# Four stacked graph layers on one core: the running maxima five pairs ahead, three blocks' softmax terms spread by TensorE, two PSUM banks for turned adjacency, and layer 1's buffers in other pools

## The chip, the cores and the metric

The kernel runs on one core of one Trainium2 chip. The metric is the device time of one execution in microseconds. Engine names are those of the profile: PE is TensorE's matmul and PEld its weight load, DVE is VectorE, ACT is ScalarE, POOL is GpSimd, SP is SyncE, which here only issues DMAs. A line number such as L326 is a line of the kernel before; the changed kernel's lines lie a few further down.

## The reference

Four residual graph layers over x (4096 x 256, float32) with one adjacency matrix adj (4096 x 4096, int32, about 0.8% ones). Each takes `h = relu(layernorm(x))`, computes a layer of h and adj, and adds it to x.

```python
# layer 0
Wh = h @ W
e = leaky(Wh @ a_src + (Wh @ a_dst).T, 0.2)
attn = softmax(where(adj > 0, e, -9e15), axis=1)
h_attn = attn @ Wh
# ... then a dense part: B, C, dt = split(Wh @ W_bcdt + b); gated MLPs of
# width 512 (fe1, fe2, W_hz, out_w, g1, g2), layer norms with gains and shifts
# layer 1
a = (adj == 1);  x += (a @ h / deg) @ W.T + b
# layer 2
h2 = h @ W
e = leaky(h2 @ a[:D] + (h2 @ a[D:]).T, 0.01)
x += elu(softmax(where(adj > 0, e, -1e12)) @ h2)
# layer 3
x += softmax(Q @ K.T + mask(adj + eye)) @ V
```

Layers 0 and 2 are additive attention: the logit of a row and a column is a leaky ReLU of one number per row plus one per column, masked by adj.

## The kernel before, in words

Rows and columns are cut into 32 tiles of 128. x stays in SBUF as `xs`. The code is written against a tile framework: buffers come from pools with a fixed count, an instruction waits by semaphore for the buffer and the data that it needs, and a scheduler orders each engine's instructions from the program order and the pools. An engine executes its instructions in its own fixed order, so a waiting instruction holds all that are behind it.

**Turned adjacency (layer 0).** A unit is a piece of 128 rows by 1024 columns of adj. `load` fetches it by POOL as bf16 (L479; 512 KB are read as int32, 256 KB written); `fresh` turns it with eight TensorE transposes into a PSUM bank (`cT`, L488), and ACT maps it with an exponential to a code in SBUF (`turned`, L493). There are 128 units. The codes also go to DRAM (`codesT`, L513), from where layers 1 to 3 read them back. `FRESH = 8` says how many pairs ahead of the running pair units are turned.

**Additive attention (class `Attention`, layers 0 and 2).** Rows are processed in blocks: layer 0 in two blocks of two row tiles and then seven of four, layer 2 in eight of four. Columns go in pairs of two tiles, 16 pairs a block (`PPB`). Three things happen for every pair, in one loop (`run`):

- `reach(n + PPB + LEAD)` takes, for the *next* block, the running minimum of code minus column term over two column tiles (L273, L275 on DVE). It gives each row's largest logit. After the block's last pair `top` turns it on TensorE (L289), computes two numbers a and b per row (L292 to L297 on DVE), turns those (`abT`, L299), and spreads them over all partitions: by a write to DRAM and a read back as a broadcast on SP's queue (L313, L314), or, for block 0 of layer 0 alone, by small matmuls against `picks` (L307) and two copies.
- `logits` makes the pair's logits y: two DVE operations with a and b (L326; ACT copied b to PSUM at the block's start, L324), then POOL subtracts the code (L330).
- Three pairs later (`lag`), ACT applies exp (L357) and PE accumulates: y as weights against `v`, which holds a column of ones, Wh and the column terms (L368). A 4-row pair is eight products. At a block's end DVE takes reciprocals of the row sums (L376), and ACT and DVE write the quotient (layer 0: `finish0`, L441 and L443; layer 2: `finish2`, L913 to L924).

`LEAD = 3` is the number of pairs by which the reaches run ahead: a block's last reach is done that many pairs before its first logits.

**Preparation of layer 0.** x arrives in eight loads of four tiles, alternating between SP and ACT (L605). `weights` loads W and the vectors a by ACT's queue and computes the columns W·a on DVE (L236). `block0` then centers x (L620, L624), takes statistics, turns x on TensorE (L145), multiplies by W (L154), and does the first reaches; beside it, adjacency units are loaded and turned.

**Dense part.** Eight blocks of 512 rows. Its late weights are loaded by `keep` in the last attention block into slots of the pool `l0_kept`, in the groups and at the pairs listed in `LATE`. Its intermediates lie in the pool `l0_d`. The last steps of a block are layer norm, POOL's multiply by ln_g (L861) and addition (L862).

**Layer 1.** `gather(t)` reads codes (L988), DVE turns them to 0/1 masks `eq` (L995) and PE multiplies (L1006). ACT counts degrees from adjacency loads (L173, L180). `reach2` prepares layer 2: `weights2` loads layer 2's weights by POOL, and its columns are again computed at L236. Pools that are opened here are laid over those that the dense part has closed.

**Layer 2** runs the same class over codes read from DRAM (`stored`, L901) into seven buffers, with two buffers for the tiles of its finish. **Layer 3** (from about 2021 us on) is ordinary attention.

Of the kernel before, what the change touches and what calls it, by code (L numbers as in the profile page):

```python
# [11 lines left out]
F32 = mybir.dt.float32  # L12
BF16 = mybir.dt.bfloat16
# [5 lines left out]
PSUM = bass.MemoryType.PSUM  # L19
DRAM = bass.MemoryType.DRAM  # L20

P = 128
# [19 lines left out]
def kernel(ctx: ExitStack, tc: tile.TileContext, w: dict, out: bass.AP):  # L42
    nc = tc.nc
    x, adj = w["x"], w["adj"]
    N, D = x.shape
# [146 lines left out]
    class Attention:  # L192
        def __init__(self, es, tag, slope, lag, n_y, blocks, turned, finish):
            self.tag, self.slope, self.lag, self.n_y = tag, slope, lag, n_y
            self.turned, self.finish = turned, finish
            self.blocks = [{"at": at, "n": n} for at, n in blocks]
            vp = es.enter_context(tc.tile_pool(name=f"{tag}_sd", bufs=1))
            self.sdst = vp.tile([P, NT], F32, name="sdst")
            self.cdst = vp.tile([P, NT], F32, name="cdst")
            self.own_dst, self.held = None, False  # L200
            self.ab_d = [
                dram.tile([2, n, P], F32, name=f"{tag}_ab_d{k}") for k, (_, n) in enumerate(blocks)
            ]
            self.picks = None
            self.small = es.enter_context(tc.tile_pool(name=f"{tag}_small", bufs=4))
            self.row_p = es.enter_context(tc.tile_pool(name=f"{tag}_rows", bufs=2))
            self.ps_run = es.enter_context(tc.tile_pool(name=f"{tag}_run", bufs=1, space=PSUM))
            self.ps_top = es.enter_context(tc.tile_pool(name=f"{tag}_top", bufs=1, space=PSUM))
# [9 lines left out]
        def weights(self, wp, work, wm, a_srcs, eng):  # L218
# [5 lines left out]
            a2 = wp.tile([P, 2 * D], F32, name="a2")  # L224
            at = 0
            for a in a_srcs:
                n = a.shape[0]
                eng.dma_start(
                    out=a2[:, at : at + n],
                    in_=a.rearrange("s o -> (s o)").partition_broadcast(P),  # L230
                )
                at += n
            for k in range(KD):
                for v in range(2):
                    junk = work.tile([P, D], F32, tag="junk", name="junk")
                    nc.vector.tensor_tensor_reduce(  # L236
                        junk, w2[:, k, 0:D], a2[:, ts(v, D)], 1.0, 0.0, ALU.mult, ALU.add,
                        w2[:, k, D + v : D + v + 1],
                    )
            self.w2 = w2  # L240
# [40 lines left out]
        def top(self, b):  # L281
# [139 lines left out]
    LEAD = 3  # L421
    FIRST = 8
    FRESH = 8
    with ExitStack() as l0:
# [10 lines left out]
        with ExitStack() as es:  # L435
# [13 lines left out]
            def turned_of(k, q):  # L449
# [4 lines left out]
            att = Attention(es, "l0", 0.2, 3, 8, cuts, turned_of, finish0)  # L454
# [4 lines left out]
            att.picks = picks.tile([4, 4, P], F32, name="picks")  # L459
            nc.vector.tensor_copy(  # L460
                att.picks,
                ident[0:4, 0:4].rearrange("k (v o) -> k v o", o=1).broadcast_to([4, 4, P]),
# [3 lines left out]
            ps_c = es.enter_context(tc.tile_pool(name="ps_c", bufs=1, space=PSUM))  # L466
# [41 lines left out]
            def ahead(n):  # L508
# [84 lines left out]
            with ExitStack() as ps_:  # L593
# [6 lines left out]
                load(4)  # L600
                att.weights(
                    wp, work, w["L0_gnn_W"], (w["L0_gnn_a_src"], w["L0_gnn_a_dst"]), nc.scalar
                )
                for b in range(NB):
                    (nc.scalar if b % 2 else nc.sync).dma_start(  # L605
# [4 lines left out]
                def block0(b):  # L610
# [16 lines left out]
                    rs = rstd_of(small, mv, BT, "pl")  # L627
                    load(2 * b + 6)
# [19 lines left out]
        with ExitStack() as es:  # L648
            d = es.enter_context(tc.tile_pool(name="l0_d", bufs=1))
# [54 lines left out]
            def hidden(z, g, b):  # L704

                zT = d.tile([P, KI, BW], F32, tag="zT", name="zT", bufs=2)
# [13 lines left out]
            def dense(b):  # L720
# [45 lines left out]
                t1 = d.tile([P, BT, DI], F32, tag="t", name="t", bufs=2)  # L766
# [20 lines left out]
                sz = d.tile([P, KI, BW], F32, tag="sz", name="sz")  # L787
# [20 lines left out]
                henh = d.tile([P, BT, D], F32, tag="henh", name="henh")  # L808
# [16 lines left out]
                comb = d.tile([P, 2 * KD, BW], F32, tag="comb", name="comb")  # L825
# [10 lines left out]
                t2 = d.tile([P, BT, DI], F32, tag="t", name="t", bufs=2)  # L836
# [110 lines left out]
    with ExitStack() as es:  # L947
# [104 lines left out]
        def weights2():  # L1052
            att2.weights(one2, two2, w["L2_gnn_W"], (w["L2_gnn_a"],), nc.gpsimd)
# [287 lines left out]
```

## Time and profile before

| what | value |
|---|---|
| median of three runs | 2996.88 us (2996.64 to 3000.27) |
| profiled execution, its own time | 2998.89 us |
| its span, first to last instruction | 2997.0 us |
| busy PE / PEld | 2864.1 us (96%) / 2334.0 us |
| busy DVE / ACT / POOL | 1878.5 / 1282.4 / 954.4 us |
| mean granted TensorE clock | 0.989 |
| moved by DMA | 239.41 MB, 80 GB/s |

The stages in the span: preparation of layer 0 until 68 us, its two small blocks until 170, its seven large blocks until 624, the dense part until 1228, layer 1 until about 1530, layer 2's attention from 1538 to 2018, layer 3 to the end.

Busy time says which engine limits a stretch, a wait says which work an engine stood for; idle time of an engine that limits nothing costs nothing. Waits are listed with the waiting instruction, what released it, the sum in us, how often, and the longest. In the timeline a row is a run of like instructions: start, length, engine, line, operation, tiles, count, and in brackets the idle time before it and its releaser.

### The profile page before, as it was taken

The numbers are of one execution on the slowest core, as the hardware profiler recorded it, in microseconds if no ns is written. First come the engines' busy times: TensorE is split into PE (matmuls) and PEld (weight loads), VectorE is DVE, ScalarE is ACT, GpSimd is POOL, SyncE is SP. The second block draws the span as 40 slices with busy tenths as digits, with TensorE's granted clock in tenths as the row PEclk, the third lists the DMA queues.
The fourth block names the chain that finished last, engine by engine and source line by source line (L and its number), as shares of the span: only waits on it lengthen the run. The fifth ranks groups of instructions, "written<-read, shape, count | busy, mean of one in ns | idle before, by whom it ended". The sixth has DMA issues, their size and how long they took to land.

```text
span 2997.0 us, 35132 instructions
## 1 busy us (share of the span) xinstructions
PE 2864.1 (96%) x13357; PEld 2334.0 (78%) x13357; DVE 1878.5 (63%) x3456; ACT 1282.4 (43%) x1961; POOL 954.4 (32%) x718
## 2 busy tenths in 40 slices
PE   6989999999999999899999999999999999999999
PEld 5778888866555666687877788888888888888888
DVE  5877666425555554477688788646766566566653
ACT  5765656459997223793163444333212112111211
POOL 4666665534554333220044655550000000000000
PEclk9999999999999999999999999999999999999999
DMA  6966665245553000496332222101111111111100
GB/s 145 213 147 128 132 133 136 67 64 77 78 78 53 8 8 8 122 241 174 123 148 85 78 78 78 43 12 61 64 44 54 38 34 62 39 34 62 34 8 8
DMA packets 109473, 239.41 MB, mean 80 GB/s; under 512 B 10780, under 2 KB 31256, under 8 KB 100600
## 3 DMA queue, kind: packets, MB, share of 16 engines
q1 hardware_dynamic: 68936, 165.44, 15.9%
q0 software_dynamic: 37696, 69.11, 15.4%
q10 hardware_dynamic: 2672, 2.62, 0.3%
q8 instruction: 105, 1.72, 0.2%
q14 instruction: 64, 0.52, 0.1%
HBM read 266.42 MB, written 37.81 MB: 102 GB/s over the span
## 4 chain that ended last, share of the span: by engine, by line
PE 63%; ACT 9%; issue 8%; POOL 7%; DVE 7%; DMA 5%; POOLq 0%; ACTq 0%; DVEq 0%; SPq 0%
PE acc L368 16%; PE acc L1273 15%; PE s L154 15%; PE mm L154 9%; PE acc L1006 5%; POOL y L330 4%; ACT sign L180 4%; DVE run L275 3%; DVE y L326 2%; DMA a<-in_adj_dram 1%; DMA ab_row<-l_ab_d 1%; ACT y L357 1%; DMA turned<-codesT 1%; ACT turned L493 1%; PE q_ps L154 1%
## 5 line engine op out<-in xcount | busy, mean ns | idle before, releaser
L368 PE MATMUL acc<-v,y 128*128 128x257 f32 x4096 | 932.8, 386 | 24.5 <-ACT hp L917 16.0
L368 PEld LDWEIGHTS acc<-v,y 128*128 128x128 f32 x4096 | 774.6, 192 | 139.6 <-ACT hp L917 21.3
L330 POOL TENSOR_TENSOR y<-y,turned 128x1024 f32<-128x1024 f32 (+1 forms) x272 | 550.0, 2036 | 315.5 <-DVE y L326 269.4
L357 ACT ACTIVATE y<-y,sdst 128x512 f32<-128x512 f32 (+1 forms) x544 | 350.8, 689 | 357.3 <-POOL y L330 357.2
L326 DVE SCALAR_TENSOR_TENSOR y<-ab_row,cdst,b 128x512 f32<-128x512 f32 (+1 forms) x544 | 366.4, 710 | 168.8 <-PE acc L368 105.4
L1273 PE MATMUL acc<-v,y 128*128 128x257 f32 x2048 | 454.5, 380 | 0.4 <-DVE rden L1281 0.4
L154 PE MATMUL s<-qT,hT 128*128 128x256 f32 x2048 | 445.2, 379 | 0.7 <-ACT qT L1221 0.7
L1266 ACT ACTIVATE y<-y 128x1024 f32<-128x1024 f32 x128 | 132.2, 1055 | 714.3 <-DVE y L1265 710.1
L154 PEld LDWEIGHTS s<-qT,hT 128*128 128x128 f32 x2048 | 389.2, 190 | 54.0 <-ACT qT L1221 1.4
L1273 PEld LDWEIGHTS acc<-v,y 128*128 128x128 f32 x2048 | 387.3, 190 | 55.7 <-issue 0.8
L180 ACT ACTIVATE sign<-a,limits 128x1024 bf16<-128x1024 bf16 x256 | 293.8, 1148 | 27.2 <-DMA a<-in_adj_dram 21.6
L1235 DVE SCALAR_TENSOR_TENSOR y<-code,s 128x512 f32<-128x512 bf16 x256 | 175.8, 687 | 100.9 <-PE s L154 100.7
L275 DVE SCALAR_TENSOR_TENSOR run<-turned,dst,run 128x512 f32<-128x512 bf16 x248 | 186.7, 753 | 42.1 <-DMA turned<-codesT 37.4
L275 DVE SCALAR_TENSOR_TENSOR run<-turned,v,run 128x512 f32<-128x512 bf16 (+1 forms) x279 | 192.9, 691 | 24.2 <-ACT turned L493 18.5
L1265 DVE TENSOR_TENSOR y<-y,top 128x1024 f32<-128x1024 f32 x128 | 146.2, 1214 | 43.0 <-PE top L1259 43.0
L1242 DVE TENSOR_TENSOR mx<-mx,y 128x512 f32<-128x512 f32 x224 | 154.9, 691 | 7.4
L493 ACT ACTIVATE turned<-cT,log_wide 128x1024 bf16<-128x1024 bf16 x128 | 140.9, 1101 | 30.9 <-PE cT L488 30.6
L1006 PE MATMUL acc<-early,eq 128*128 128x512 f32 x512 | 129.1, 401 | 10.7 <-issue 9.1
L154 PE MATMUL mm<-kept 128*128 128x512 f32 x288 | 136.7, 612 | 1.6 <-DVE kept L687 0.8
L173 POOL DMA_DIRECT2D a<-in_adj_dram x128 | 76.1, 596 | 190.8 <-ACT sign L180 158.2
L1006 PEld LDWEIGHTS acc<-early,eq 128*128 128x128 f32 x512 | 96.8, 190 | 34.3 <-issue 11.2
L1006 PE MATMUL acc<-late,eq 128*128 128x512 f32 x512 | 122.5, 391 | 0.0
(233 smaller groups left out, 2988.9 us busy)
## 6 DMA issues: line engine op xcount, KB each, us to landing
turned<-codesT SPq DMA_DIRECT2D x36, 1024.0 KB
adj_t<-in_adj_dram POOLq DMA_DIRECT2D x128, 256.0 KB, 4.6
codesT<-turned SPq DMA_DIRECT2D x32, 1024.0 KB
a<-in_adj_dram POOLq DMA_DIRECT2D x128, 256.0 KB, 4.7
code<-codesT SPq DMA_DIRECT2D x128, 256.0 KB
code<-codesT SPq DMA_DIRECT2D x64, 512.0 KB
ab_row<-l_ab_d SPq DMA_DIRECT2D x15, 512.0 KB
xt<-in_x_dram SPq DMA_DIRECT2D x8, 512.0 KB
```

The costliest lines, as they stand in the source:

```text
L154: nc.tensor.matmul(out=ps, lhsT=lhsT_of(k), rhs=rhs_of(k), start=(k == 0), stop=(k == n - 1))
L180: nc.scalar.activation(sign, self.came[g], AF.Sign, bias=limits[:, v : v + 1], accum_out=over[:, t, v, q : q + 1],)
L275: nc.vector.scalar_tensor_tensor(st["run"], code, dst, st["run"], ALU.subtract, ALU.min)
L326: nc.vector.scalar_tensor_tensor(y[:, :, k, :], st["ab"][:, 0, :, :], self.cdst[:, c + k : c + k + 1], st["b"], ALU.add, ALU.max,)
L330: nc.gpsimd.tensor_tensor(y, y, mask[:, :, c % QT : c % QT + 2, :], ALU.subtract)
L357: nc.scalar.activation(y[:, :, k, :], y[:, :, k, :], AF.Exp, bias=self.sdst[:, c + k : c + k + 1],)
L368: nc.tensor.matmul(out=acc, lhsT=y[:, r, k, :], rhs=self.v[:, c + k, 0 : D + 1], start=(c + k == 0), stop=(c + k == NT - 1),)
L493: nc.scalar.activation(ct.rearrange("p c i -> p (c i)"), ps, AF.Exp, scale=math.log(UNIT / WIDE), bias=log_wide,)
L1006: nc.tensor.matmul(out=acc, lhsT=eqs[c // (NT // 2)][:, ts(c % (NT // 2), P)], rhs=v1[c // BT][:, c % BT, :, :], start=(c == 0), stop=(c = ...
L1235: nc.vector.scalar_tensor_tensor(y[:, :, c : c + 2, :], st["code"][:, :, c : c + 2, :], -BIG / UNIT, ps, ALU.mult, ALU.add,)
L1242: nc.vector.tensor_tensor(mx, mx, y[:, :, c : c + 2, :], ALU.max)
L1273: nc.tensor.matmul(out=accs[r], lhsT=st["y"][:, r, c, :], rhs=v3[:, c, :], start=(c == 0), stop=(c == NT - 1),)
```

## The change

- `LEAD` is 5 instead of 3, in layers 0 and 2.
- The first three blocks of layer 0 (2, 2 and 4 rows) get a and b over all partitions by TensorE matmuls, a and b one after the other in a PSUM tile each; the others still go through DRAM.
- The turned adjacency, the turned minima, `abT` and the spread share one PSUM pool with two banks under one tag; before, the turned adjacency had one bank and the others another.
- At the start: two adjacency loads come ahead of the weights instead of four, all x loads go to SP, and the W·a columns are a function of their own (`columns`), called after block 0's statistics. Layer 2 calls `columns` right after its weights, and its row of a shares the tag of the tile `h`.
- In the dense part `zT`, `t`, `sz`, `henh` and `comb` lie in a new pool `l0_old`, opened ahead of `l0_d`; in `LATE` the first group and the last change places. Layer 1's tiles, laid out over the closed pools, come to lie elsewhere.
- Layer 2 has eight buffers for loaded codes instead of seven, and one for the finish instead of two.

```diff
-            self.picks = None
+            self.picks, self.spread = None, 0
...
-            self.ps_top = es.enter_context(tc.tile_pool(name=f"{tag}_top", bufs=1, space=PSUM))
+            self.ps_top = ps_top or es.enter_context(
+                tc.tile_pool(name=f"{tag}_top", bufs=1, space=PSUM)
+            )
...
-            a2 = wp.tile([P, 2 * D], F32, name="a2")
+            a2 = wp.tile([P, 2 * D], F32, tag=tag, name="a2")
...
+            self.w2, self.a2 = w2, a2
+
+        def columns(self, work):
+            w2, a2 = self.w2, self.a2
             for k in range(KD):
                 for v in range(2):
                     junk = work.tile([P, D], F32, tag="junk", name="junk")
...
-            if self.picks is not None and b == 0:
-
-                ps = self.ps_top.tile([P, 2 * n, P], F32, tag="top", name="spread")
-                for k in range(2 * n):
-                    nc.tensor.matmul(
-                        out=ps[:, k, :], lhsT=self.picks[:, k, :], rhs=abT, start=True, stop=True
-                    )
+            if b < self.spread:
+
                 for v in range(2):
-                    evac(1 - v, st["ab"][:, v, :, :], ps[:, ts(v, n), :])
+                    ps = self.ps_top.tile([P, n, P], F32, tag="top", name="spread")
+                    for k in range(n):
+                        nc.tensor.matmul(
+                            out=ps[:, k, :], lhsT=self.picks[0 : 2 * n, v * n + k, :], rhs=abT,
+                            start=True, stop=True,
+                        )
+                    evac(1 - v, st["ab"][:, v, :, :], ps)
                 return
...
-    LEAD = 3
+    LEAD = 5
...
-            att = Attention(es, "l0", 0.2, 3, 8, cuts, turned_of, finish0)
+            ps_c = es.enter_context(tc.tile_pool(name="ps_c", bufs=2, space=PSUM))
+            att = Attention(es, "l0", 0.2, 3, 8, cuts, turned_of, finish0, ps_c)
...
-            att.picks = picks.tile([4, 4, P], F32, name="picks")
+            n = 2 * RB
+            att.picks, att.spread = picks.tile([n, n, P], F32, name="picks"), 3
...
-            ps_c = es.enter_context(tc.tile_pool(name="ps_c", bufs=1, space=PSUM))
...
-                    ps = ps_c.tile([P, QW], BF16, tag="cT", name="cT")
+                    ps = ps_c.tile([P, QW], BF16, tag="top", name="cT")
...
-                (1, ("fe1_w", "fe2_w")), (2, ("W_hz",)), (3, ("g1_w",)), (4, ("out_w", "g2_w")),
+                (1, ("abp_w", "out_b", "fe2_b", "g2_b", "ln_g", "ln_b", (1, BW))), (2, ("W_hz",)), (3, ("g1_w",)), (4, ("out_w", "g2_w")),
                 (6, ("fe1_b", "g1_b", (KD, BW))),
-                (10, ("abp_w", "out_b", "fe2_b", "g2_b", "ln_g", "ln_b", (1, BW))),
+                (10, ("fe1_w", "fe2_w")),
...
-                load(4)
+                load(2)
...
-                    (nc.scalar if b % 2 else nc.sync).dma_start(
+                    nc.sync.dma_start(
...
                     rs = rstd_of(small, mv, BT, "pl")
+                    if b == 0:
+                        att.columns(work)
...
+            old = es.enter_context(tc.tile_pool(name="l0_old", bufs=1))
             d = es.enter_context(tc.tile_pool(name="l0_d", bufs=1))
...
-                zT = d.tile([P, KI, BW], F32, tag="zT", name="zT", bufs=2)
+                zT = old.tile([P, KI, BW], F32, tag="zT", name="zT", bufs=2)
...
-            att2.weights(one2, two2, w["L2_gnn_W"], (w["L2_gnn_a"],), nc.gpsimd)
+            att2.weights(one2, w["L2_gnn_W"], (w["L2_gnn_a"],), nc.gpsimd, "h")
+            att2.columns(two2)
...
-        turned_p = es.enter_context(tc.tile_pool(name="l2_turned", bufs=7))
-        work2 = es.enter_context(tc.tile_pool(name="l2_work", bufs=2))
+        turned_p = es.enter_context(tc.tile_pool(name="l2_turned", bufs=8))
+        work2 = es.enter_context(tc.tile_pool(name="l2_work", bufs=1))
```

More of the change, by code (lines that the diff above doesn't have):

```diff
@@ L192, with __init__ @@
     class Attention:
-        def __init__(self, es, tag, slope, lag, n_y, blocks, turned, finish):
+        def __init__(self, es, tag, slope, lag, n_y, blocks, turned, finish, ps_top=None):
             self.tag, self.slope, self.lag, self.n_y = tag, slope, lag, n_y
@@ L216, in dst_of, with weights @@
             return self.v[:, at, D + 2] if self.own_dst is None else self.own_dst[:, at]
-        def weights(self, wp, work, wm, a_srcs, eng):
+        def weights(self, wp, wm, a_srcs, eng, tag="a2"):
             w2 = wp.tile([P, KD, D + 2], F32, name="w2")
@@ L239, in weights @@
                     )
-            self.w2 = w2
         def project(self, b, hT, psm, rs=None):
@@ L457 @@
             picks = es.enter_context(tc.tile_pool(name="picks", bufs=1))
-            att.picks = picks.tile([4, 4, P], F32, name="picks")
+            n = 2 * RB
+            att.picks, att.spread = picks.tile([n, n, P], F32, name="picks"), 3
             nc.vector.tensor_copy(
                 att.picks,
-                ident[0:4, 0:4].rearrange("k (v o) -> k v o", o=1).broadcast_to([4, 4, P]),
+                ident[0:n, 0:n].rearrange("k (v o) -> k v o", o=1).broadcast_to([n, n, P]),
             )
@@ L599 @@
                 first_p = ps_.enter_context(tc.tile_pool(name="l0_first", bufs=FIRST))
-                load(4)
+                load(2)
                 att.weights(
-                    wp, work, w["L0_gnn_W"], (w["L0_gnn_a_src"], w["L0_gnn_a_dst"]), nc.scalar
+                    wp, w["L0_gnn_W"], (w["L0_gnn_a_src"], w["L0_gnn_a_dst"]), nc.scalar
                 )
                 for b in range(NB):
-                    (nc.scalar if b % 2 else nc.sync).dma_start(
+                    nc.sync.dma_start(
                         out=xs[:, ts(b, BT), :],
@@ L764, in dense @@
                 yield
-                t1 = d.tile([P, BT, DI], F32, tag="t", name="t", bufs=2)
+                t1 = old.tile([P, BT, DI], F32, tag="t", name="t", bufs=2)
                 for i in range(BT):
@@ L785, in dense @@
                 a1T = yield from hidden(t1, fe_g, fe_b)
-                sz = d.tile([P, KI, BW], F32, tag="sz", name="sz")
+                sz = old.tile([P, KI, BW], F32, tag="sz", name="sz")
                 for k in range(KI):
@@ L807, in dense @@
                         yield
-                henh = d.tile([P, BT, D], F32, tag="henh", name="henh")
+                henh = old.tile([P, BT, D], F32, tag="henh", name="henh")
                 for i in range(BT):
@@ L823, in dense @@
                         yield
-                comb = d.tile([P, 2 * KD, BW], F32, tag="comb", name="comb")
+                comb = old.tile([P, 2 * KD, BW], F32, tag="comb", name="comb")
                 for k in range(2 * KD):
@@ L835, in dense @@
                 yield
-                t2 = d.tile([P, BT, DI], F32, tag="t", name="t", bufs=2)
+                t2 = old.tile([P, BT, DI], F32, tag="t", name="t", bufs=2)
                 for i in range(BT):
```

## The prediction

> **What bounds the kernel now.** I read the engine totals first, then busy time by stage, then the list of waits in each stage that the change touches.
>
> ```profile
> PE 2864.1 (96%) x13357; PEld 2334.0 (78%) x13357; DVE 1878.5 (63%) x3456; ACT 1282.4 (43%) x1961; POOL 954.4 (32%) x718
> 0.00:68.00 68.00, 45.80 (x270) 37.95 (x271) 35.27 (x142) 36.50 (x66) 28.94 (x47) 1.00 0.63 140
> 81.40:170.00 88.60, 78.63 (x515) 65.39 (x516) 71.33 (x149) 64.83 (x105) 56.63 (x64) 0.94 0.91 212
> 170.00:624.00 454.00, 436.99 (x2474) 375.76 (x2473) 286.68 (x471) 243.04 (x336) 278.98 (x193) 1.00 0.50 113
> 1228.00:1240.00 12.00, 2.92 (x10) 2.46 (x11) 5.21 (x10) 1.39 (x2) 3.42 (x6) 0.71 1.02 311
> 1538.00:2018.00 480.00, 459.49 (x2082) 396.51 (x2083) 352.96 (x583) 199.62 (x307) 276.42 (x131) 0.98 0.18 63
> 2021.00:2997.00 976.00, 967.66 (x4496) 845.99 (x4496) 601.66 (x932) 162.09 (x187) 5.67 (x4) 1.00 0.13 42
> ```
>
> The columns are the stretch, its length, busy PE, PEld, DVE, ACT and POOL, the granted clock, the DMA share and GB/s. TensorE is the bound nearly everywhere, and the change takes no matmul of the main products away. So a gain can come only from PE's gaps: 22 us before 68, 17 in 170:624, 20.5 in 1538:2018, 9 around 1230, plus time at half clock. From 2021 on there is no edit and no gap: that third stays.
>
> **Start (0:68).** All x loads go to SP, the a·W columns come after block 0's statistics, two adjacency loads precede them instead of four.
>
> ```profile
> PE tp L145 <- ACT xs L620: 16.3, 1, 16.3
> ACT L620 <- issue: 14.4, 1, 14.4
> DVE junk L236 <- DMA a<-in_L_gnn_a_src_dram: 8.0, 1, 8.0
> ...
> 2.33 12.01 ACTq L605 DMA_DIRECT2D xs<-in_x_dram  x4
> ```
>
> PE starts at 16.3, behind ScalarE's first centering of x; ScalarE is held to 14.4 by issuing four x loads, 12.01 us for four; VectorE waits 8.0 and then 2.4 us for the a rows before it finishes block 0's statistics. A rule speaks against the first edit: the Trainium skill's "DMA: Bandwidth & Descriptors", section "Issuing engines are not separate DMA queues", says that all DMAs end on the same 16 engines and that spreading issues saves only the issuing sequencer's time, usually small. By it moving four loads is worth four issues at the 0.5 us of ACT's other loads, 2 us. The row has 3 us an issue, on the engine that PE waits for, so I follow the row. After: ACT is free at about 2.3, its table load (1.28) done by 4; one column product still stands ahead of the statistics on VectorE, so they run from about 8.4 to 11.5; PE starts at 11 to 12.5. Then eight blocks of 5.2 to 5.8 us of PE each follow (first products of the last blocks are 5.2 to 5.8 apart), where before block 1's came 8.2 after block 0's. That puts the end of the preparation at 59 to 61, not 68: **8 us**. Bounds: 13 if block 1's x no longer waits (3.7 us before); 2 by the rule. SP's queue then holds eight issues at 1.26 us (its four took 5.04), 10 us; what is behind it, the weights of the dense stage, is not read before 520.
>
> **First blocks (68:170).** Blocks 0 to 2 spread a and b by TensorE; the adjacency turns through two PSUM banks, shared with the small transposes. With one bank a unit goes PE, then ACT (1.10 us), then PE: 1.8 to 2.2 us a lap; with two it is ACT's 1.1. From the last reach (68.9) to the first product (81.4) 12.5 us pass; afterwards eight units at 1.1 plus the spread (16 matmuls; the 8 of before took 2.07) and a softmax step are again about 12: 1 us. The spread takes two writes and two row loads off SP's queue, and its two copies from PSUM (0.37 and 0.42 in block 0, about double with four rows) go to ACT and VectorE; the two row loads took 5.7 and 10.4 us, and PE stood 5.0 us at 160 behind a turned unit. Against this stand two things. The DMA share of this stretch is 0.91, so loads of 512 KB, every 2.2 us, set a floor near the 88.6 us. And the instruction order of the changed kernel bunches 12 units between block 1's last product and block 2's first: 12 x 1.1 = 13.2 us of ACT beside 12 x 0.45 = 5.4 of PE, a bubble of 8. I take 1.5 us gain for the whole; bounds +10 (bubble with nothing won) and −10.
>
> **Steady blocks of layer 0 (170:624, seven of 4 rows).** The maxima run five pairs ahead.
>
> ```profile
> DVE y L326 <- ACT b L324: 46.6, 6, 9.2
> ...
> PE cT L488 <- ACT turned L493: 7.6, 9, 2.0
> PE acc L368 <- ACT xs L443: 6.0, 8, 1.5
> ```
>
> A pair costs PE 3.97 us with its unit of transposes (its transposes start at 240.46, 244.43, 248.40, 252.37 in the timeline): 16 x 3.97 = 63.5 a block, against 66.5 to 69.4 measured for the five that still transpose. So some 3 to 5 us a block is gap. Each block VectorE waits on average 46.6/6 = 7.8 us for b, which comes through a DMA round trip after the maximum; pairs of y then run late and PE's three-pair lag empties. Two more pairs of lead are 2 x 3.97 = 7.9 us: the size of the wait. In the new VectorE order two y and six reach steps (6 x 0.75 = 4.5) fill that place. PSUM release of acc (6.0 in all) stays; the second bank takes most of the 7.6. I take 2.3 us x 5 = **11.5**; bounds 5 and 18.
>
> **Layer 0 to 1.**
>
> ```profile
> PE acc L1006 <- issue: 9.1, 1, 9.1
> DVE junk L236 <- DMA a<-in_L_gnn_a_dram: 6.3, 1, 6.3
> ```
>
> PE stands 9.1 us and then has half clock for 10.24 us (three windows of 3.41 by the clock column), 5.1 lost. The masks eq stand on VectorE behind a column product whose row landed at 1234.3; the code loads went out at 1223.5, after POOL's multiply L861. In the new pools the masks lie on tiles done earlier, and the column product comes after them; but the code loads still lie on `l0_kept` slots and still wait for the same multiply, and the 1.02 DMA share says that their 2 MB need until about 1232 anyway. The count loads (1229.8) go out earlier. So I take 3.5 us of the stall and one window's 1.7: **5**; bounds 0 (loads last anyway) and 9. The free half of the edit, other late weights first, I cost at nothing: they are issued near 568 and first read near 630, 60 us of cover; without it, a 1 MB load, 5 us.
>
> **Layer 2 (1538:2018).** Lead 5, eight buffers for loaded codes, one for the finish.
>
> ```profile
> DVE run L275 <- DMA turned<-codesT: 37.4, 12, 3.6
> ...
> PEld acc L368 <- ACT hp L917: 21.3, 13, 3.1
> PE acc L368 <- ACT hp L917: 16.0, 13, 2.7
> ```
>
> Pure PE is 16 x 3.52 = 56.3 us a block, and blocks take 60.3 to 61.5. At each block's end VectorE stands 3.5 us for a codes load, with the reciprocals that free the accumulators queued behind it; ACT's finish is late, and PE waits 2.2 to 2.9 us and again 0.5. With eight buffers the load goes out a block's quarter earlier, and with lead 5 it is wanted earlier by two pairs (7 us), but no longer beside the block's end. The waits sum to 16.0 + part of 4.2 (a small transpose in block 0). The clock adds to it:
>
> ```profile
> 1661.60:1663.10 1.50, 0.70 (x2) 0.30 (x2) 1.50 (x6) 1.50 (x3) 0.44 (x1) 1.00 0.00 0
> 1663.10:1666.50 3.40, 3.20 (x8) 2.56 (x9) 3.26 (x5) 1.90 (x3) 1.16 (x1) 0.50 0.00 0
> ```
>
> After gaps of 2.69 and 0.45 us the clock is 0.50 for 3.4 us, 1.7 lost; the same in four more blocks. The skill's "TensorE: Matmul & The Clock Gate", section "What's actually happening", lets the clock drop after at least one idle window of about 3.4 us. Read as an idle gap of that length, these gaps cost no clock and the sum is 16; by the trace it is up to 16 + 5 x 1.7 = 24.5. The measurement decides. I take three quarters of the gaps (12) and half the clock (4): **16**; bounds 6 and 26. The one buffer of the finish is used once in 58 us: nothing; if a finish met the next, its 1.6 us multiply-add would wait.
>
> **Sum.** 8 + 1.5 + 11.5 + 5 + 16 = 42 us. The profiled execution took 2998.9 (span 2997.0 and 1.9 around it), 2.0 above the median of 2996.88. So 2956.9 on its scale, **2955 us** on the median's.
>
> **Rivals.**
> - *Half of it comes.* The first 170 us are held by DMA and the bunched units (0 instead of 9.5, or 4 worse), the code loads of layer 1 do not move (0 instead of 5: there the change would not do what it says), layer 0 keeps half: 42 − 9.5 − 5 − 6 to −10 leaves 17 to 22, 2975 to 2980. For it: the 0.91, the unmoved release. Against: the gaps of layer 2 do not depend on either.
> - *Lockstep in layer 0, slower.* Units are turned 8 pairs ahead. With lead 3 a reach has two pairs of cushion to the unit it reads; with lead 5 every fourth reach reads a unit turned in its own step, and the next pair's y are queued behind it on VectorE, POOL's subtraction behind those, ACT's exp and PE behind that. A stop is one bank lap, 2.2 us. PE has three pairs in hand, 11.9 us, less 0.74 x 2 + 2.13 + 1.33 = 4.9 for the chain: 7 us of slack. Only if stops pass that, as when ACT is late with exp as well, do they reach PE: 4 stops x 2.2 x 5 blocks = 44, less 42 + 11.5 lost of the gain: 42 − 11.5 − 44 = 13.5 slower, **3010**. For it: 14.2 us that reach already waits for turned units. Against: the slack and the second bank.
> - *More than that.* All bounds good: −13 −8 −18 −7 −24 = 70, 2927.
>
> **Chances.** Main case (2935 to 2966) 0.58; more 0.08; half 0.20; nothing measurable 0.05; slower 0.09. Faster by over 0.2% (6 us; about what a measurement can tell) is 0.86, within it 0.05, slower 0.09. The range that holds 8 in 10 takes the main case, the half case and most of the larger one: 2928 to 2984.
>
> **What would show it.** Start: PE's first transpose at 11 to 12.5, the preparation's end near 60, first product near 72. Layer 0: "DVE y <- ACT b" from 46.6 to under 15, blocks at 64.5. Layer 1: the wait before its first product at 5 to 6. Layer 2: "PE acc <- ACT hp" from 16.0 under 5, "DVE run <- DMA turned" from 37.4 under 12, the stage at 464, the clock at 1.00. Wrong if "DVE run <- ACT turned" grows past 40 in layer 0 (lockstep), if the first product is still near 80, or if layer 2's blocks stay above 60 with another releaser.

## The result

The changed kernel takes 2991.62 us in the median of 12 runs (2983.71 to 2998.02), the kernel before 2996.76 (2993.84 to 3000.68): ratio 0.9981, 95% interval 0.9973 to 0.999. It is faster by 5 us, not by 42. The profiled execution took 2988.39 us with a span of 2986.5, 10.5 less than that of before. The runs of the changed kernel scatter more than those of before, so single profiles are read by stage and the totals by medians.

The large blocks of layer 0 and layer 2's attention, in the same columns as for the kernel before and with the bounds moved to where these stages now lie:

```profile
164.00:618.40 454.40, 438.00 (x2475) 377.53 (x2473) 301.76 (x474) 243.03 (x336) 280.97 (x192) 0.99 0.50 116
1524.60:2012.20 487.60, 459.78 (x2085) 396.16 (x2086) 368.65 (x588) 197.50 (x307) 273.79 (x134) 0.98 0.17 62
```

The preparation is 9.5 us shorter, and layer 2, where 16 us were to be won, is longer: 487.6 us. From the timelines of both profiles, each point against the same one before (blocks are counted from 0 in each layer):

| point in the program | before | changed | gained so far |
|---|---|---|---|
| end of the preparation | 67.9 | 58.4 | 9.5 |
| first product of block 0, layer 0 | 81.35 | 71.13 | 10.2 |
| end of block 1 | 160.04 | 144.43 | 15.6 |
| first product of block 2 | 168.59 | 164.04 | 4.6 |
| end of layer 0's attention | 624.80 | 618.36 | 6.4 |
| first product of layer 1 | 1237.08 | 1223.49 | 13.6 |
| first product of layer 2 | 1538.26 | 1524.60 | 13.7 |
| end of layer 2's block 3 | 1781.00 | 1765.12 | 15.9 |
| end of layer 2's block 5 | 1901.39 | 1897.81 | 3.6 |
| end of layer 2 | 2018.43 | 2012.22 | 6.2 |
| first `q_ps` product of layer 3 | 2065.99 | 2055.74 | 10.3 |

Two drops give most of the gain back: 11 us before block 2 of layer 0, and 12 us in blocks 4 and 5 of layer 2. The lists of waits of the changed kernel, for the start, the large blocks of layer 0, the entry of layer 1, and layer 2, in this order:

```profile
PE tp L145 <- ACT xs L627: 9.6, 1, 9.6
...
PE acc L374 <- ACT xs L449: 8.5, 6, 2.9
...
PE abT L304 <- DVE ab L302: 7.8, 6, 1.4
DVE y L332 <- ACT b L330: 7.5, 6, 4.2
...
PE acc L1017 <- issue: 3.3, 1, 3.3
...
DVE run L280 <- DMA turned<-codesT: 20.5, 8, 5.2
...
PE acc L374 <- ACT hp L928: 16.7, 10, 5.2
...
DVE run L278 <- DMA turned<-codesT: 12.9, 3, 6.0
```

VectorE's wait for b went from 46.6 to 7.5 us, as forecast, yet the large blocks gained only 1.9 us together (456.2 to 454.3, from block 2's first product to the end of layer 0's attention). In the kernel before, PE's own waits in that stretch (170 to 624) were these four:

```profile
PE cT L488 <- ACT turned L493: 7.6, 9, 2.0
PE acc L368 <- ACT xs L443: 6.0, 8, 1.5
PE abT L299 <- DVE ab L297: 3.2, 5, 0.7
PE acc L368 <- DVE rden L376: 0.2, 1, 0.2
```

None is for a late y, so VectorE's wait for b did not reach PE. In layer 2 the wait for codes came to the first reach of a block (L278), and PE's wait for the finish did not shrink (16.0 before, 16.7 now).

The drop in layer 2, in the timeline around the end of block 4:

```profile
1824.57 18.20 SPq L912 DMA_DIRECT2D turned<-codesT  x2
...
1832.08 0.76 DVE L278 TENSOR_SCALAR run<-turned,dst 128x512 f32<-128x512 bf16 x1 [6.02 <-DMA turned<-codesT]
...
1836.30 0.16 DVE L382 RECIPROCAL rden<-acc 128x1 f32<-128x1 f32 x1
...
1836.50 0.56 ACT L928 ACTIVATE hp<-acc,minus,rden 128x256 f32<-128x256 f32 x1 [6.41 <-DVE rden L382]
...
1837.11 1.23 PE L374 MATMUL acc<-v,y 128*128 128x257 f32 x2 [5.20 <-ACT hp L928]
```

Read it from the top: the codes load goes out at 1824.57 (the 18.20 us of this row span two issues), when POOL has finished with the ring's oldest buffer. VectorE comes to the first reach on these codes at 1826 and stands 6.02 us. The reciprocals of the block that PE has ended at 1831.5 are behind that reach in VectorE's order; so the finish on ACT is late, no accumulator is free, and PE stands 5.20 us. The load itself was slow here: it landed 7.4 us after its issue, where such a load takes 4.8 in the median.

The drop before block 2 of layer 0, PE's timeline:

```profile
149.71 0.61 PE L495 MATMUL cT<-identb,adj_t 128*128 128x128 bf16 x8 [0.40 <-ACT turned L500]
...
159.76 1.03 PE L495 MATMUL cT<-identb,adj_t 128*128 128x128 bf16 x8 [2.73 <-DMA adj_t<-in_adj_dram]
163.21 1.03 PE L495 MATMUL cT<-identb,adj_t 128*128 128x128 bf16 x8 [2.41 <-DMA adj_t<-in_adj_dram]
```

Twelve units stand in a row, one per 1.0 us, paced by ACT; the last three wait for adjacency loads as well, and the first product of block 2 follows at 164.04.

### The profile page after: what moved, and what is told of

Its sections match the earlier page's. It is cut to its first block, busy times and chain, and to the rows that moved or that the text cites. A ratio compares the mean times of both kernels' runs of the same rounds, so it can differ in the third digit from the quotient of the medians.

```text
span 2986.5 us, 35207 instructions
## 1 busy us (share of the span) xinstructions
PE 2862.8 (96%) x13381; PEld 2332.3 (78%) x13381; DVE 1906.5 (64%) x3458; ACT 1279.1 (43%) x1963; POOL 948.4 (32%) x718
## 4 chain that ended last, share of the span: by engine, by line
PE 70%; ACT 8%; DVE 7%; issue 6%; POOL 6%; DMA 3%; POOLq 0%; SPq 0%; ACTq 0%; DVEq 0%
PE acc L374 20%; PE acc L1285 15%; PE s L154 15%; PE mm L154 9%; PE acc L1017 8%; POOL y L336 3%; ACT sign L180 3%; DVE y L332 2%; DVE run L280 1%; PE cT L495 1%; DMA turned<-codesT 1%; PE q_ps L154 1%; ACT t L710 1%; ACT y L363 1%; DMA a<-in_adj_dram 1%
## 5 line engine op out<-in xcount | busy, mean ns | idle before, releaser
L374 PE MATMUL acc<-v,y 128*128 128x257 f32 x4096 | 929.6, 385 | 27.2 <-ACT hp L928 16.7
```

What stands on the lines that cost most here:

```text
L374: nc.tensor.matmul(out=acc, lhsT=y[:, r, k, :], rhs=self.v[:, c + k, 0 : D + 1], start=(c + k == 0), stop=(c + k == NT - 1),)
```

## The experiments

All ratios are against runs of the kernel before on the same chip. Differences in us are between medians that may come from different chips, on which the kernel before took 2995.7 to 2998.3 us; those under 3 us tell nothing. Every kernel is the changed one with the edit shown, unless said otherwise.

**One bank for turned adjacency** (its own pool, the small tiles in another):

```diff
-            ps_c = es.enter_context(tc.tile_pool(name="ps_c", bufs=2, space=PSUM))
-            att = Attention(es, "l0", 0.2, 3, 8, cuts, turned_of, finish0, ps_c)
+            ps_c = es.enter_context(tc.tile_pool(name="ps_c", bufs=1, space=PSUM))
+            att = Attention(es, "l0", 0.2, 3, 8, cuts, turned_of, finish0)
```

> The changed kernel with the PSUM arrangement of before: one bank for turned adjacency, another for the small turned tiles and the spread. In the instruction order the bunch of 12 units between block 1 and block 2 is gone. Theory (the shared two-bank pool makes the bunch, and the bunch costs the start's gain): block 2's first product at 155 to 158 us instead of 164, and the kernel 6 to 10 us faster than the changed one, about 2983. Rival (the adjacency loads are the floor of the first 165 us): block 2 still begins at 163 to 165 and the time stays within 3 us of 2991.6. Second rival (two banks also save PE's lap in the steady blocks): blocks 2 to 6 longer by 2 us each, the kernel slower by up to 5.

2995.0 us, ratio 0.9991 (0.9984 to 0.9998). Block 2 began at 161.5, 1.1 us after block 1's end instead of 19.6: the bunch is gone. But block 2 itself took 76.1 us to the next block's first product instead of 66.1: from block 0's first product to block 3's it is 155.9 us instead of 159.0, so the bunch costs about 3 us there. And the preparation ended at 67.3 although PE's first transpose was at 9.7. In its waits up to 60 us:

```profile
ACT xs L627 <- DVE pl_mv L123: 15.1, 6, 4.4
PE cT L495 <- ACT turned L500: 5.5, 3, 4.7
```

With one bank a unit's transposes wait for ACT to empty the bank, and ACT is held by the centering of a later block. None of my three theories had that.

**The old start**, two banks kept (four adjacency loads first, x on both queues, columns first):

> The changed kernel with the start of before: four adjacency loads first, x loads alternating between SP and ACT, the columns of W and a ahead of block 0's statistics; two PSUM banks, spread and lead stay. Theory (the start edits bring PE's first transpose from 16.3 to 9.6, the second bank only keeps it): first transpose at 16, preparation's end at 64 to 66, but the first 165 us end within 3 us of the changed kernel's 164.0, because the bunch of units there waits for adjacency anyway: time within 4 us of the changed kernel. Rival (the start's gain goes through): 6 to 9 us slower.

2999.5 us, ratio 1.0007 (0.9996 to 1.0018), 7.9 slower than the changed kernel: the rival. The first transpose came at 17.6, the preparation ended at 67.6, block 2 began at 174.5. So for the end of the preparation (67.9 before) the early start and the second bank each bring under 1 us alone and 9 us together, and that gain goes through. The three edits of the start were undone together; what each is worth was not measured.

**Only block 0 spread by TensorE** (`att.spread` 1 instead of 3):

> The changed kernel with only block 0 spread by TensorE; blocks 1 and 2 take the DMA round trip again. In the instruction order the bunch before block 2 is 32 and 16 transposes instead of 96. Theory (the bunch is what costs): block 2's first product 3 to 6 us earlier unless its row load (10.4 us in the kernel before) takes over, total 0 to 5 us faster than the changed one. Rival (spreading by TensorE is itself the gain of the first 165 us): slower by 5 to 8 us.

2997.4 us, ratio 1.0 (0.9991 to 1.0008), 5.7 slower than the changed kernel: the rival. Block 2 began at 162.1, 1.9 earlier, but between blocks 2 and 3 PE stood 5.1 us for an accumulator, and the two blocks took 143.3 us instead of 133.1.

**Lead 3 in layer 0:**

```diff
-    LEAD = 5
+    LEAD, LEAD2 = 3, 5
```

> The changed kernel with lead 3 in layer 0 and lead 5 in layer 2. Theory (PE's three pairs in hand covered the wait for b, so the longer lead gave layer 0's large blocks nothing and only moved their gap): blocks 2 to 6 within 1 us of 66 to 67 each, DVE waits for b back at 40 us or more, time within 4 us of the changed kernel. Rival 1 (lead 5 does gain there, and something else lost it): slower by 6 to 12. Rival 2 (lead 5 costs, by reaches that stand on freshly turned units): faster by 5 or more.

2989.9 us, ratio 0.9972 (0.9962 to 0.9982): within 2 us of the changed kernel, as the theory had it. In the stretch of the large blocks:

```profile
DVE y L332 <- ACT b L330: 48.8, 6, 9.5
PE acc L374 <- ACT xs L449: 16.3, 10, 3.8
```

The wait for b is back at 48.8 us and the total is the same. But two things cancel in it: block 2 began at 155.7, 8.3 us earlier (no bunch of 12), and the large blocks took 463.4 us instead of 454.3. Blocks 3 to 6 took 67 to 73 us from first product to first product (forecast 66 to 67; the changed kernel 67 to 69). PE waited for no y there either; its waits for accumulators grew, and after them it ran 17 us at a granted clock of 0.50, against 5.6 in the changed kernel. So this run alone doesn't show that the longer lead is worth nothing; that the wait for b was no wait of PE is shown by PE's own list, above.

**The old order of the late weights** (fe1 and fe2 at pair 1):

> The changed kernel with the old order of the late weights (fe1 and fe2 at pair 1, the small rows at pair 10); the new pools stay. Theory (six row loads moved ahead of the bias rows on SP's queue, so VectorE waits 3.0 us for a bias row at 495 with the reciprocals behind it, and PE 2.9): that wait of PE goes to about 0.5, block 7 of layer 0 begins 2.5 us earlier, the kernel is 2 to 3 us faster up to there. Rival (the bias row is late for the longer lead): the wait stays at 3. For layer 1 the layout decides: if the code loads' slots move, its first product may come up to 4 us earlier or later; by my reading within 2.

2989.5 us, ratio 0.9974 (0.9962 to 0.9985). VectorE's wait for the bias row fell from 3.0 to 1.9 us, PE's before block 7 from 2.9 to 2.1. My theory had 0.5 there: a small part of the wait belongs to the order, most does not. The total can't tell it from the changed kernel.

**The dense part in one pool**, with that old order:

> The changed kernel with the dense part's tiles back in one pool and the old order of the late weights. Theory (in the new layout layer 1's masks and count loads no longer stand behind the last layer norm's tiles): PE's wait before layer 1's first product goes from 3.3 back to 8 to 9 us, the way from layer 0's dense part to layer 1 from 605 to 611 or 612, the kernel 5 to 7 us slower than the changed one. Rival (the order of the column product on VectorE does it, not the layout): under 2 us slower.

2993.0 us, ratio 0.9989 (0.9982 to 0.9997), 1.4 slower than the changed kernel, which looks like the rival; but it is 3.5 slower than the kernel with the same order of late weights, the closer comparison, and there the intervals barely overlap. PE's wait before layer 1's first product (1222.23) stayed short, 2.4 us, but a second stop came 11 us later:

```profile
1231.67 1.15 ACT L180 ACTIVATE sign<-a,limits 128x1024 bf16<-128x1024 bf16 x1 [11.17 <-DMA code<-codesT]
...
1233.43 2.93 PE L154 MATMUL mm<-w_L_gnn_WT,hT 128*128 128x256 f32 x6 [4.29 <-ACT hT L107]
```

ACT stands 11.17 us for the first adjacency load of the degree count (its input `a`, issued at 1222.23; the row names another load), and the copy that PE needs is behind it. With the new pools the count loads go out 19 to 21 us before layer 1's first product, with the old ones at it (0.0 to 2.3 us after it). PE's stops and half clock at the entry of layer 1 were 9.1 and 10.2 us before, 3.6 and 3.4 in the changed kernel, 7.8 and 6.8 here. So the layout does bring the count loads forward and takes this second stop away. From the end of layer 0's attention to layer 2's first product the kernel before took 913.5 us, the changed one 906.2, this one 910.1 (the others with the new pools and eight y buffers in layer 0: 904.7 to 909.7). What the layout did not shorten is the wait before the first product. By the order of VectorE's instructions that is the work of the column product of layer 2, which in the kernel before stood ahead of the masks and waited 6.3 us for its row; now its row shares the tile `h` and the product comes after the masks. That edit was not run by itself.

**Layer 2: lead 3** (eight code buffers, one finish buffer stay):

> The changed kernel with lead 3 in layer 2 (still eight code buffers and one buffer of the finish) and lead 5 in layer 0. Theory (with lead 5 a block's first reach stands directly on its codes load, so VectorE waits 4.6 to 6.0 us at the ends of blocks 3 and 4 and PE 4 to 5): these two blocks come down from 66 to 60 or 61 us, the kernel is 8 to 12 us faster than the changed one, about 2981. Rival 1 (the two long blocks come from the single finish buffer): no change, within 3 us. Rival 2 (lead 5 is a gain in layer 2): slower by 3 or more.

2986.6 us, ratio 0.9966 (0.9954 to 0.9978), 5 faster than the changed kernel; layer 2 took 479.4 us. Blocks 1 and 2 took 57.5 and 58.4 us, but 4 and 5 still 64.5 and 63.7: lead 5 is not the main thing that makes these two long.

**Layer 2: seven code buffers, lead 5:**

> The changed kernel with seven code buffers in layer 2 instead of eight; lead 5 and the single finish buffer stay. In VectorE's order the next block's first reach comes after the reciprocals again; with eight buffers it stands before them from block 3 on. Theory (the eighth buffer moved the first reach onto a load issued just before it, with the reciprocals behind): the wait of VectorE's first reach on DMA falls from 12.9 us to under 4, blocks 4 and 5 of layer 2 come from 66 to 61 or less, the kernel is 8 to 14 us faster than the changed one, about 2980. Rival 1 (lead 5 itself is what puts reaches on loads): blocks 4 and 5 stay above 64. Rival 2 (the single finish buffer): the same, no change.

3014.4 us, ratio 1.0054 (1.0035 to 1.0072). My theory, that the eighth buffer does the harm, fell: without it layer 2 took 509 us, with all blocks but the last two at 63 to 67.

```profile
DVE run L280 <- DMA turned<-codesT: 52.4, 18, 5.8
```

Lead 5 holds two more pairs of codes, so that with seven buffers more of the loads go out late: VectorE waited for codes 18 times at this line instead of 8.

**Layer 2 as before** (lead 3, seven buffers, two of the finish):

> The changed kernel with all three edits of layer 2 undone (lead 3, seven buffers, two of the finish). Theory: layer 2's blocks at 60 to 61.5 as in the kernel before, 480 us for the stage, 7 to 8 us faster than the changed one (about 2984); lead 5 with seven buffers is better than this by 1 to 6. Rival (layer 2's longer blocks come from what layer 1 leaves behind, not from its own edits): blocks 4 and 5 stay above 64. Open besides: the 4.0 us stop of PE after layer 2's last block, which the changed kernel lost; if the single finish buffer took it away it comes back here and not in the kernel with seven buffers and one.

2985.0 us, ratio 0.9954 (0.9938 to 0.997); layer 2 took 481.3 us. This is the changed kernel's gain outside layer 2, 13 us. The stop after layer 2's last block did not come back, so neither the layer's buffer counts nor its lead had removed it. The single finish buffer was never changed alone.

**Layer 2: lead 2, eight buffers:**

> The changed kernel with lead 2 in layer 2; eight code buffers and the single finish buffer stay. In VectorE's order the next block's first reach stands behind the block's reciprocals in every block. Theory (a long block is one whose first reach stands on its codes load ahead of the reciprocals): no block over 61.5 us, VectorE's waits on code loads under 20 us in all, layer 2 from 487.6 to 468 to 476 us, the kernel 10 to 18 us faster than the changed one, 2974 to 2982. Rival (with a shorter lead the wait for b comes onto PE's path, as the prediction had it for lead 3): blocks of 61 to 63, 484 us or more, faster by under 4.

2996.2 us, ratio 1.0005 (0.9998 to 1.0012): the rival. The largest new wait in layer 2:

```profile
ACT abT_sb L306 <- PE abT L304: 44.2, 7, 7.9
```

The waits on code loads fell to 12.3 us in all, and the late maximum takes their place: blocks of 58 to 63 us, layer 2 at 494.

**Layer 2: six y buffers** (eight code buffers, lead 5):

```diff
-    att2 = Attention(l2, "l2", 0.01, 3, 8, cuts2, None, finish2)
+    att2 = Attention(l2, "l2", 0.01, 3, 6, cuts2, None, finish2)
```

> The changed kernel with six y buffers in layer 2 instead of eight, lead 5 and eight code buffers stay. VectorE then can't run y ahead, and in its order the first reach stands behind the reciprocals in every block. Theory: as for lead 2, blocks of 58 to 60, layer 2 at 470 to 478 us, 9 to 17 us faster than the changed kernel. Rival (fewer y in hand let PE run dry at block ends, where VectorE is late): blocks of 61 or more.

2965.3 us, ratio 0.9898 (0.9884 to 0.9913), 26 faster than the changed kernel. Layer 2 and its waits:

```profile
1529.00:1989.20 460.20, 452.16 (x2085) 392.14 (x2086) 364.89 (x588) 197.04 (x306) 274.62 (x134) 1.00 0.18 65
...
DVE y L332 <- PE acc L374: 62.1, 40, 2.5
...
DVE run L280 <- DMA turned<-codesT: 3.7, 8, 0.7
PE acc L374 <- ACT hp L928: 3.7, 7, 0.8
```

And the same place as shown above, the end of block 4:

```profile
1814.96 0.32 SPq L912 DMA_DIRECT2D turned<-codesT  x1
...
1816.05 0.17 DVE L382 RECIPROCAL rden<-acc 128x1 f32<-128x1 f32 x1 [0.65 <-PE acc L374]
...
1819.74 0.75 DVE L278 TENSOR_SCALAR run<-turned,dst 128x512 f32<-128x512 bf16 x1 [0.51 <-DMA turned<-codesT]
```

The load goes out 4.3 us before VectorE asks for it, not 1.5, and the reciprocals come first: VectorE stands 0.51 us. My reading: with eight y buffers VectorE and POOL rush through a block's first pairs as soon as b is there, so the pair that frees a code buffer and the reach that needs the next one come close together; with six they are paced by PE. For it: VectorE's wait for products to free a y buffer is 62.1 us, in the changed kernel 44.2, and at the first product of a block, from block 1 on, it has made 5 pairs of that block's y, there 6 or 7. It does not say why lead 5 is needed besides.

**The ninth code buffer beside six y:**

> As the kernel with six y buffers, and the room used for a ninth code buffer. In VectorE's order the first reaches stand ahead of the reciprocals from block 4 on, by up to seven reaches. If the load's lateness is what costs (a ring of eight frees a slot only when the block before last's quarter is done), the ninth buffer lets the load go out a quarter earlier: waits on code loads under 10 us, blocks at 58 to 59, 468 to 474 us. If the order itself costs, whatever the load: blocks 4 to 6 at 62 or more.

2966.7 us, ratio 0.9903 (0.9888 to 0.9918): blocks at 56.3 to 59.3 us though reaches stand ahead of the reciprocals there. So that order does no harm by itself when the loads are in time. With six y the ninth buffer adds nothing.

**Six y with lead 3, and six y in the kernel before:**

> The changed kernel with six y buffers and lead 3 in layer 2, eight code buffers. Told apart: how much of the 26 us that six y buffers brought at lead 5 needs the lead. If the lead does it (five pairs of reaches interleave with six pairs of y): blocks of 60 to 61, layer 2 at 478 or more, 10 to 16 us slower than the kernel with six y and lead 5. If the y count does it, by keeping VectorE from filling eight buffers before it turns to the reaches: blocks of 58, within 5 us of it.

2984.2 us, ratio 0.9962 (0.995 to 0.9974): 19 us slower than with lead 5. VectorE waited 36.4 us for codes, and four of the loads went out only when it already stood. Pacing by PE does not explain that.

> The kernel before, with six y buffers in layer 2 and nothing else changed (lead 3, seven code buffers). If the y count alone does it: layer 2 from 480 to 466 to 472 us, 8 to 14 us faster than the kernel before. If it takes the lead and the eighth buffer besides: within 4 us of the kernel before.

2999.0 us, ratio 1.0004 (0.9997 to 1.0011): no change, with 48.2 us of waits on codes. With eight code buffers, lead 3 took 2986.6 us with eight y and 2984.2 with six, lead 5 took 2991.6 and 2965.3: each alone brings nothing or loses, both together bring 21 us. Five more kernels with six y and lead 5 have layer 2 at 459 to 462 us. Why the two need each other is open. Six y and lead 5 on seven code buffers were not run.

**Six y in both layers:**

> The changed kernel with six y buffers in both attention layers, lead 5. In the instruction order the bunch of 96 transposes before block 2 of layer 0 is cut to 16 and 48. If layer 0 has the same fault as layer 2: block 2's first product at 156 to 160 instead of 164 and large blocks at 64 to 65 instead of 65.4 to 67, 5 to 9 us faster than with six y in layer 2 alone (about 2958). If layer 0 is bound by its adjacency units instead (four of each block's reaches read a unit turned in their own step): within 2 us of 2965, or slower.

3004.1 us, ratio 1.0019 (1.0011 to 1.0028), 39 slower than with six y in layer 2 alone. Layer 0's attention ended 60 us later, and the dense part took 17 less; VectorE waited 45.3 us for freshly turned units. The smaller y pool also let layer-1 counting start inside layer 0's attention (POOL waits 65.6 us for its signs there), so the two are not told apart.

**Six y in layer 2 and lead 3 in layer 0; that with units nine pairs ahead; lead 4 in layer 0:**

> The changed kernel with six y buffers in layer 2 (lead 5 there) and lead 3 in layer 0. With lead 3 in both respects of layer 0 the earlier run of this kind ended layer 0 0.7 us after the changed kernel and ended 1.7 us sooner. If lead 5 is no gain for layer 0: 2962 to 2968, as with lead 5. If the bunch before block 2 was really saved by lead 3 and lost again by chance later: 5 us or more faster, about 2959.

2961.5 us, ratio 0.9881 (0.9866 to 0.9896): 3.8 below lead 5, which the intervals do not separate. It is the lowest median here, together with the next.

> Six y buffers in layer 2, lead 3 in layer 0, and units of adjacency turned nine pairs ahead instead of eight. In the instruction order the bunch before block 2 is 16 transposes, and every reach of layer 0 has three pairs to the unit that it reads. If layer 0's gaps come from bunches and from reaches that read fresh units: block 2's first product near 156 as with lead 3 and eight, large blocks under 67, 2 to 6 us faster than 2961.5, about 2958. If they come from the accumulators' release and the small transposes alone: within 2 us of 2961.5.

2961.7 us, ratio 0.9879 (0.9862 to 0.9897). Block 2 began at 151.3, 12.7 earlier than in the changed kernel, and layer 0 ended at 621.8, 3.4 later: what is won before block 2 is given back by block 7. In its large blocks PE ran 27 us at clock 0.50.

> Six y buffers in layer 2 and lead 4 in layer 0, units eight pairs ahead. In the order 47 transposes are bunched between blocks 0 and 1 and 39 before block 2. If the lead is what shortens layer 0's large blocks (65.4 us with 5, 67 to 69 with 3) and the bunch what loses the start, 4 lies best: about 2958. If the ends of blocks 6 and 7 take back what comes before, as in all kernels with the new start so far: 2961 to 2965, like 3 and 5.

2983.9 us, ratio 0.9957 (0.9944 to 0.997), 18.5 slower than lead 5, against both theories. In its large blocks:

```profile
DVE run L280 <- ACT turned L500: 47.9, 16, 4.9
```

A reach waits for the unit just turned, and the y behind it are late. At the end of block 3 (295.8):

```profile
296.77 0.23 DVE L382 RECIPROCAL rden<-acc 128x1 f32<-128x1 f32 x2
297.87 1.33 ACT L363 ACTIVATE y<-y,sdst 128x512 f32<-128x512 f32 x2 [1.88 <-POOL y L336]
...
301.17 0.45 ACT L449 ACTIVATE xs<-acc,rden 128x256 f32<-128x256 f32 x1
301.77 1.62 PE L374 MATMUL acc<-v,y 128*128 128x257 f32 x3 [5.13 <-ACT xs L449]
```

The reciprocals are ready by 298, but ACT's quotient, which frees the accumulator, stands behind the exponentials of those late y in ACT's order, and PE stands 5.13 us.

## Why the prediction was wrong

It said 2955 us in a range of 2928 to 2984; 2991.6 came. The steps, in the order of its sum:

- **Start, 8 us: right in size.** PE's first transpose came at 9.6 (11 to 12.5 forecast), the preparation ended at 58.4 (near 60). The row was the better guide than the rule on DMA issues: ScalarE began at 5.5 us instead of 14.4, so 8.9 earlier and not 2; the old start as a whole cost 7.9 us. But the gain was put to the start edits alone; the two runs show that it needs the second bank too. So the size was in part luck. (The end at 59 to 61 does not follow from eight blocks of at most 5.8 us after 12.5, which make 58.9; first transpose to end took 48.8 us. Eight issues on SP took 13.3 us, not 10.)
- **First blocks, 1.5 us: wrong.** 5.7 us were lost from the first product to block 2. The bubble of 12 units that the text named cost 11 us and not 8 (19.6 from block 1's end to block 2's start, 8.6 before), as adjacency loads were late for its last three (5.7 us of waits); the gains set against it were 5.4 us, where 1.5 + 8 = 9.5 had been counted. A unit took 1.0 us, as forecast (1.1). The outer bound, 10 us lost, held.
- **Large blocks of layer 0, 11.5 us: the step that failed in kind.** It is "pairs of y then run late and PE's three-pair lag empties": it took VectorE's wait for b, 7.8 us a block, for PE's gap. PE's own waits of before, shown above, add up to 17.0 us, the whole of PE's gap in this stretch (454.00 less 436.99), and none is for a late y: the three pairs in PE's hand covered the wait for b. It went to 7.5 in all and the blocks gained 1.9 us together. The second bank did take its part, the 7.6 (none is left), but the other two grew: "PE acc <- ACT xs" from 6.0 to 8.5, "PE abT <- DVE ab" from 3.2 to 7.8. The prediction used the three pairs as slack against the lockstep rival, and not here. Its gap of 3 to 5 us a block was also too large, since a pair with its unit was taken as 3.97 us (63.5 a block), where PE is busy about 65 and stands 2.7 on average.
- **Layer 0 to 1, 5 us: right**, 7.2 on the profile. Of its two causes the layout brings the count loads forward, as forecast (the kernel with one pool has the second stop); that the column product behind the masks shortens the first wait is argued from the order.
- **Late weights, nothing: about 1 us lost by the profile.** They were costed by when they are read, and not by what they pass on SP's queue.
- **Layer 2, 16 us: wrong in sign.** 7.5 us were lost. The failed step is "it is wanted earlier by two pairs, but no longer beside the block's end". At the ends of blocks 3 and 4 it was wanted just there, 1.4 and 1.5 us after its issue. The gain that was named is real: with six y buffers the stage fell from 480 to 460 us, the clock from 0.98 to 1.00, and "PE acc <- ACT hp" from 16.0 to 3.7, under the 5 that was forecast. One reading was off: of the five drops of the clock before, four follow gaps at a block's end and one (1577.8) the 4.24 us of the small transpose in block 0; after a fifth block end with 2.26 and 0.36 us there was none.
- **After layer 2, nothing: 4 us gained.** The prediction's stretches skip from 2018 to 2021, where the stop began. PE no longer stood 3.85 us before layer 3's first transpose. In the kernel before, POOL's load of that layer's weights waited 13.2 us there for a product; in the changed one that wait is not in the list. Which edit did it is not settled; it was not the pools of the dense part, nor layer 2's buffers or lead.

The slower rival, lockstep on freshly turned units, did not come at lead 5 (21.6 us of such waits), but it exists: lead 4 has it with 47.9 us. That it sits at 4 and not at 5 was not foreseen by counting pairs; presumably the scheduler's order of the instructions decides it.

In part open: why layer 0 gives back by block 7 whatever is won before block 2. In the three runs with lead 3, two of them with six y buffers in layer 2 and one of these with units nine pairs ahead, PE waits longer for accumulators at the ends of blocks, and the clock then takes its share: 17, 17 and 27 us at 0.50 in the large blocks, against 5.6 in the changed kernel and 2.9 in the one before. At half the clock about half of it is lost: by this estimate 6 and 11 us more than in the changed kernel, of the 9 and 16 by which these blocks are longer with eight and with nine pairs. Why the accumulators come free later there is not settled; no run took these waits away.

## What to carry to other kernels

A wait of an engine that is not the bound is no gain until you have counted what the bound engine has in hand; the quick test is to list what the bound engine itself waited for, and to see whether its sum leaves any room. When a look-ahead is lengthened, follow the ring of buffers behind it: what frees a slot, how long the load takes, and how soon the next user asks; here fewer buffers of y and a longer lead had to come together, and neither alone brought a gain. Where instructions are put in order by a scheduler, a buffer count is a change of order, so compare the order of the waiting instruction and of what stands behind it before believing a sum.

## What the runs showed of the hardware

In the changed kernel a 1 MB load of codes landed in 4.8 us in the median, and one was waited for until 7.5 us after its issue, with a DMA share of only 0.17 in the stage. With the four x loads off ScalarE's queue, where their issues had taken 12.01 us, its table load began at 5.5 us instead of 14.4.

The clock fell after gaps of about 2 us. In layer 2 of the kernel before it was 0.50 for 3.4 us after four block ends at which PE had stood 2.04 to 2.69 us and again 0.40 to 0.47; after a fifth, with 2.26 and 0.36, it stayed at 1.00. With six y buffers, where no gap at a block's end is over 0.82 us, it did not fall at any of them.
